# One more recurrent step of the last two batches with seven products instead of eight, and a new planned order

## The chip, the core and the metric

The kernel runs on one core of a Trainium2 chip. The metric is the device time of one execution in microseconds (us). The kernel before was timed three times: 1460.43, 1460.33 and 1458.93 us, median 1460.33. One further execution was recorded by the hardware profiler.

## The reference

Sixteen batches of 1024 nodes with 128 features pass two layers, each with a residual and a layer norm. Layer 0 is an attention layer over a fixed 0/1 adjacency matrix; layer 1 is a gated recurrent network of five steps on the same matrix. Cut to what matters here:

```python
# layer 0
h = x @ others_weight
att = softmax(where(adj > 0, leaky_relu(u1[pairs] + u2[pairs]), NEG), axis=1)
x = layernorm(x + att @ h + x @ self_weight)
# layer 1: five times, h starts as x
m  = adj @ h                               # per batch, 1024 x 1024 by 1024 x 128
u  = h @ u3.T
z  = sigmoid([m, m] @ w3.T + u);  r = sigmoid([m, m] @ w4.T + u)
hv = tanh([m, m] @ w5.T + (r * h) @ u5.T)
h  = (1 - z) * h + z * hv
# end
out = layernorm(x + h)
```

## The kernel before

Everything lies in halves of 128 x 512 floats: `hT` is the state of a batch, features on the partitions and nodes along a row, in two halves. The batches go in pairs, q = 0 to 7. The work of pair q and step s is one *message* stage and then *gates*.

**Messages (from L1045).** They need the state with nodes on the partitions, split in two parts that TensorE multiplies one after the other: a rounded part (`split`, the cast at L609 on ScalarE) and the rest (the subtraction at L613 on VectorE). One product is eight matmuls of 128 x 512 (L621). A *plain* stage makes eight products for a pair. A stage in *Strassen's form* makes seven, out of sums of the four halves of both batches (L1083) and of four sums of the adjacency's quarters, which were made once; both batches of the pair are then needed at once, and their results are put together by copies on ScalarE (L1141, L1143) and additions on VectorE (L1151). The set `PLAIN` at L28 lists the plain stages as (pair, step).

**Gates (from L1163).** For each half of each batch: a matmul of the state (L1189), a copy of it (L1192), two matmuls of the message (L1199) for r and z, their tanh (L1202), r times the state (L1209, VectorE), two matmuls for the candidate (L1215, L1216), its tanh (L1221), and three VectorE operations, less, times and sum (L1224, L1227, L1230), the last of which writes the state. All these matmuls are in float32.

**Leaving a step (from L1283).** The new state must be turned. Either TensorE does it, four transposes of 128 x 128 for a half (L571), and the split reads PSUM; the set `TURNED` at L32 lists the (pair, step) for which this is so. Or VectorE turns blocks of 32 x 32 (L579), four DMAs write the half to DRAM in the right places (`away`, L589), and one DMA brings it back (`back`, L597). After the last step the half gets the input added (L1332 or L1262) and is normalised.

**A norm (L522).** Statistics on VectorE (L527, L529), four or five small operations on GpSimd with the power -1/2 (L533 to L543), and four scalings on ScalarE (L548).

**The order.** No engine decides it while the program runs. The class `Plan` records every piece of work with its engine, a length in ns, a rank and the tiles that it reads and writes. `order` then plays the work through once: an engine that is free takes the ready piece of lowest rank. What follows from a piece is ready after its length and a *lag*, which stands for semaphores and, for a DMA, for the time to landing. The instructions are issued in the order that comes out; each engine, and the queue of DMAs on SyncE, works through its own list strictly in turn. Ranks are `10 * pair + 4.2 * step` plus an offset by kind of work, from the table `D` at L303; a batch before its first step has `rank0` at L317. `LATE` (L31) is the lag of the DMA that brings a half back. `LATER` (L29) sets the second batch of the last pair back by 1.5 in plain stages only. So a changed lag or offset moves instructions on every engine.

Of the kernel before, what the change touches and what calls it, by code (L numbers as in the profile page):

```python
# [24 lines left out]
SHIFT = 40.0  # L25
LOW, HIGH = -20.0, 100.0
TINY = 1e-30
PLAIN = {(0, 0), (0, 1), (0, 2), (7, 2), (7, 3), (7, 4)}  # L28
LATER = 1.5  # L29
AHEAD = range(4, 8)  # L30
LATE = 3001  # L31
TURNED = {(0, 0), (0, 1), (7, 2), (7, 3)}  # L32
IDLE = 60


# [102 lines left out]
def kernel(  # L138
# [79 lines left out]
    def exact(pools):  # L218
# [67 lines left out]
        plan = Plan({tag: k[0] for tag, k in kinds.items()})  # L286
# [13 lines left out]
            plan.add("SP", *a, **k)  # L300


        D = dict(m=-0.8, pu=1.4, u=0.8, pr=0.8, pz=1.2, r=1.7, pv=1.0, z=1.3, hv=-0.4, h=1.2, tr=1.6, o=6.6, ln=2.9)  # L303
        D.update(out=4.4, l1=-9, l2=-4, l3=-2, l4=-4, l5=-7, l6=-1.5, l7=-1, l8=-2)

        def on_pe(b, what):

# [7 lines left out]
            return 10 * (b // 2) + 4.2 * s + (LATER if b == B - 1 and plain(b // 2, s) else 0)  # L315

        def rank0(b):  # L317
            return 10 * (b // 2) - 1 * (1 - b % 2) + -1.0 - 6 * (b // 2 == 1)

        def sign(b):  # L320

            return 1 if b % 2 else -1
# [17 lines left out]
        def early_loads():  # L340
# [28 lines left out]
            writes=[(boot, "early"), (ws, "early"), (x0, "early"), (("xt", 1), "early"), *((t, "early") for k in staged for t in k)],  # L369
# [149 lines left out]
                dve(V, 1 + c / 4, sum_, reads=[*y, *more], writes=[(("tab",), c, n)])  # L519


        def layernorm(key, g, rank, after, src, dst, write, sg=1, short=False, later=()):  # L522
            stats, mv, rstd = ("stats", *key, g), ("mv", *key, g), ("rstd", *key, g)

            def look():
                for j in range(4):
                    nc.vector.bn_stats(T(stats)[:, j, :], src(j))  # L527
                for j in range(4):
                    nc.vector.bn_aggr(T(mv)[:, j, :], T(stats)[:, j, :])  # L529

            def power():
                mean, var, r = T(mv)[:, :, 0], T(mv)[:, :, 1], T(rstd)
                nc.gpsimd.tensor_scalar(r[:, 0, :], var, EPS, None, ALU.add)  # L533
                nc.gpsimd.tensor_tensor(r[:, 0, :], r[:, 0, :], mhalf[:, 0:4], ALU.pow)
                if short:
                    if sg < 0:
                        nc.gpsimd.tensor_scalar(r[:, 0, :], r[:, 0, :], -1.0, None, ALU.mult)
                elif sg > 0:
                    nc.gpsimd.tensor_scalar(r[:, 1, :], mean, -1.0, None, ALU.mult)
                    nc.gpsimd.tensor_tensor(r[:, 1, :], r[:, 1, :], r[:, 0, :], ALU.mult)  # L540
                else:
                    nc.gpsimd.tensor_tensor(r[:, 1, :], mean, r[:, 0, :], ALU.mult)
                    nc.gpsimd.tensor_scalar(r[:, 0, :], r[:, 0, :], -1.0, None, ALU.mult)  # L543

            def scale():
                r = T(rstd)
                for j in range(4):
                    nc.scalar.activation(  # L548
                        dst(j), src(j), AF.Identity, bias=r[:, 1, j : j + 1], scale=r[:, 0, j : j + 1]
                    )  # L550

            def scale_short():
                for j in range(4):
                    nc.vector.tensor_scalar(
                        dst(j), src(j), T(mv)[:, j, 0:1], T(rstd)[:, 0, j : j + 1], ALU.subtract, ALU.mult
                    )

            after = after if isinstance(after, list) else [after]
            dve(1100, rank, look, reads=after, writes=[(stats, 0), (mv, 0)])
            plan.add("POOL", 2301 if short else 3001, rank, power, reads=[(mv, 0)], writes=[(rstd, 0)])  # L560
            if short:
                dve(900, rank, scale_short, reads=[*after, (mv, 0), (rstd, 0)], writes=[write])
            else:
                act(1250, rank, scale, reads=[*after, *later, (mv, 0), (rstd, 0)], writes=[write])
# [66 lines left out]
        def layer0(b):  # L631

            first = rank0(b) - (60 if b == 0 else 0)
            rank = first + D["l1"]
            xt, hx, pb, u, us, uu, ud = (
                ("xt", b), ("hx", b), ("pb", b), ("u3", b), ("us", b), ("uu", b), ("ud", b)
            )
# [6 lines left out]
            yT, y0, yd = ([(k, b, g) for g in range(2)] for k in ("yT", "y0", "yd"))  # L644
# [46 lines left out]
            if b >= 2:  # L691
# [6 lines left out]
                    reads=[(u, 0), (u, 1), (("ident",), 0)],  # L698
                    writes=[(put, 0)],
# [8 lines left out]
                    reads=[(us, 0)],  # L708
                    writes=[(ud, 0)],
# [5 lines left out]
                    reads=[(ud, 0)],  # L715
                    writes=[(pb, 0), (pb, 1)],
                    lag=3000,
# [245 lines left out]
            for g in range(2):  # L963
                rank = rank0(b) + D["l5"]

                def y(g=g):
                    return T(yT[g])

                t = ("ps", "t", b, "y", g)
                if on_pe(b, "y"):  # L970
                    transposes(y, [(yT[g], 0)], t, rank)
                else:
                    k, d, t = (x + (b, "y", g) for x in (("T",), ("D",), ("F",)))
                    turn(k, y, [(yT[g], 0)], rank)
                    away(k, d, rank)
                    back(d, t, rank)

                def src(j, t=t, flat=on_pe(b, "y")):
                    return T(t)[:, j * P : (j + 1) * P] if flat else chunks(T(t))[:, j]

                def dst(j, g=g, flat=on_pe(b, "y")):
                    c = T(y0[g])[:, j, :]
                    return c if flat else c.rearrange("p (a j) -> p a j", a=4)

                layernorm(("y", b), g, rank0(b) + D["l6"], (t, 0), src, dst, (y0[g], 0), sign(b))

            if not plain(b // 2, 0):

# [293 lines left out]
        def leave(b, s):  # L1282

            rank = rank_of(b, s)
            hT = ("hT", b)
            for g in range(2):

                def h(g=g):
                    return T(hT)[:, g * HALF : (g + 1) * HALF]

                k, d = ("T", b, s, g), ("X", b, s + 1, g)
                if s < STEPS - 1 and on_pe(b, s):
                    t = ("ps", "t", b, s, g)
                    transposes(h, [(hT, g)], t, rank + D["tr"])
                    split(
                        ("blk", b, "h", s + 1, g),
                        lambda t=t: T(t).rearrange("p (c a j) -> p c a j", c=4, a=4),
                        [(t, 0)],
                        rank_of(b, s + 1),
                    )  # L1300
                    continue
                if s < STEPS - 1:
                    turn(k, h, [(hT, g)], rank + D["tr"])
                    away(k, d, rank + D["tr"])
                    continue

                if b >= B - 2:
                    end(b, s, g, h, rank)
                    continue

                t = ("ps", "t", b, s, g)
                if on_pe(b, s):
                    transposes(h, [(hT, g)], t, rank + D["tr"])
                else:
                    t = ("F", b, s, g)
                    turn(k, h, [(hT, g)], rank + D["tr"])
                    away(k, d, rank + D["tr"])
                    back(d, t, rank + D["o"])

                o, yd = ("o", b, g), ("yd", b, g)  # L1320
                sp(
                    450,
                    rank + D["o"],
                    lambda o=o, yd=yd: nc.sync.dma_start(T(o).rearrange("p c d -> p (c d)"), T(yd)),
                    reads=[(yd, 0), (hT, g)],
                    writes=[(o, "y")],
                )

                def last(t=t, o=o, flat=on_pe(b, s)):
                    x = T(o).rearrange("p c (a j) -> p c a j", a=4)  # L1330
                    n = T(t).rearrange("p (c a j) -> p c a j", c=4, a=4) if flat else chunks(T(t))
                    nc.vector.tensor_tensor(x, n, x, ALU.add)  # L1332

                dve(V, rank + D["o"], last, reads=[(t, 0), (o, "y")], writes=[(o, "raw")])

                def at(j, o=o):
                    return T(o)[:, j, :]

                layernorm(("o", b), g, rank + D["ln"], (o, "raw"), at, at, (o, 0), sign(b))
                plan.add(  # L1340
                    "POOL",
                    900,
                    rank + D["out"],
                    lambda o=o, g=g: nc.gpsimd.dma_start(
                        out[b].rearrange("(c p) d -> p c d", p=P)[:, 4 * g : 4 * g + 4, :], T(o)
                    ),
                    reads=[(o, 0)],
                    writes=[((o, "sent"), 0)],
                    lag=2600,
                )  # L1350
# [347 lines left out]
```

## Time and profile before

| | |
|---|---|
| median of three timed executions | 1460.33 us (1458.93 to 1460.43) |
| the profiled execution, whole time | 1468.01 us |
| its span, first to last instruction | 1466.2 us |
| TensorE idle in the span | 25.8 us |
| of it before 40 us | 3.1 us |
| of it after 1440 us | 13.4 us |
| TensorE clock granted, mean | 0.994 |
| norms: powers on GpSimd | 64, two for each batch and layer |

The profiled execution took 7.68 us longer than the median of the timed ones, and 1.8 us of it lie outside its span. A busy TensorE in this profile means a chain of matmuls without a gap between them: one product of eight matmuls advances it by 1.87 us, a float32 matmul of 128 x 512 by 0.86 us (two records), four transposes by 0.43 us. Where one instruction follows another in a view of the timeline, the difference of the starts is the time that counts, since the records of neighbours overlap.

### The profile page before, as it was taken

To read this page: it belongs to the slowest core of one execution; us is meant where nothing else is said; L and a number is where in the kernel's file an instruction comes from. 1 tells how busy PE (TensorE), PEld (TensorE's weight loads), DVE (VectorE), ACT (ScalarE), POOL (GpSimd) and SP (SyncE) were. 2 spreads that over 40 slices of the span, in tenths; PEclk is the share of its full clock that TensorE was granted. 3 is DMA by queue.
4 is the path that set the end of the run, shared out by engine and by line. 5 is a ranking of instruction groups with operands and counts; after the bars stand their busy time and mean duration, and the time that the engine had idled before them with its cause. 6 is when DMAs were issued, how large, how long until landed. Compare 5 with 4: busy or idle time off the path is not lost.

```text
span 1466.2 us, 17789 instructions
## 1 busy us (share of the span) xinstructions
PE 1440.4 (98%) x5020; PEld 902.3 (62%) x5020; DVE 1160.1 (79%) x2753; ACT 896.2 (61%) x1792; POOL 203.3 (14%) x323
## 2 busy tenths in 40 slices
PE   9999999998999999999999999999999999999996
PEld 7766656665566656666666656656566656556663
DVE  5997789868888789987888788896988877776535
ACT  5656465665657665666657576566655656664544
POOL 0311001012101150110201112011200123000201
PEclk9999999999999999999999999999999999999998
DMA  7426135554434643455434543445432554223201
GB/s 250 145 55 205 52 102 150 137 158 116 112 100 137 184 126 90 121 163 150 108 108 123 158 129 101 115 143 159 123 89 79 150 166 129 58 72 87 72 0 31
DMA packets 188032, 174.20 MB, mean 119 GB/s; under 512 B 34239, under 2 KB 137366, under 8 KB 187926
## 3 DMA queue, kind: packets, MB, share of 16 engines
q1 hardware_dynamic: 182562, 156.41, 37.8%
q0 software_dynamic: 4800, 15.73, 3.2%
q8 instruction: 41, 0.67, 0.2%
q10 hardware_dynamic: 564, 0.85, 0.2%
q14 instruction: 65, 0.53, 0.1%
HBM read 95.68 MB, written 77.24 MB: 118 GB/s over the span
## 4 chain that ended last, share of the span: by engine, by line
PE 88%; DVE 4%; DMA 2%; SPq 1%; ACT 1%; issue 1%; POOL 1%; DVEq 0%; POOLq 0%; ACTq 0%
PE ps_acc_a L621 16%; PE ps_g_r L1199 8%; PE ps_g_v L1215 8%; PE ps_g_v L1216 8%; PE gz L1199 8%; PE ps_g_r L1189 8%; PE ps_acc_c L621 8%; PE ps_acc_po L621 8%; PE ps_acc L621 5%; PE gz L621 4%; PE ps_g_ph L658 1%; PE ps_idle L419 1%; SPq L589 1%; PE ps_acc_px L925 1%; PE ps_acc_po L939 1%
## 5 line engine op out<-in xcount | busy, mean ns | idle before, releaser
L1215 PE MATMUL ps_g_v<-m,wm 128*128 128x512 f32 x320 | 163.5, 592 | 0.1
L1216 PE MATMUL ps_g_v<-r,u5h 128*128 128x512 f32 x320 | 163.4, 592 | 0.0
L1199 PE MATMUL ps_g_r<-m,wm 128*128 128x512 f32 x320 | 160.0, 593 | 2.6 <-ACT gz L1192 2.6
L1199 PE MATMUL gz<-m,wm 128*128 128x512 f32 x320 | 159.5, 592 | 0.0
L1189 PE MATMUL ps_g_r<-hT,u 128*128 128x512 f32 x320 | 153.3, 592 | 0.0
L1224 DVE TENSOR_TENSOR hv<-hv,hT 128x512 f32<-128x512 f32 x160 | 109.8, 686 | 51.5 <-ACT hv L1221 51.0
L621 PE MATMUL ps_acc_a<-tab,blk_s 128*128 128x512 f32 x544 | 148.6, 415 | 1.6 <-ACT m L1141 1.6
L1209 DVE SCALAR_TENSOR_TENSOR r<-r,hT 128x512 f32<-128x512 f32 x160 | 109.2, 685 | 51.3 <-ACT r L1202 51.0
L1202 ACT ACTIVATE r<-ps_g_r,bh 128x512 f32<-128x512 f32 x160 | 109.1, 687 | 66.4 <-PE ps_g_r L1199 66.1
L621 PE MATMUL ps_acc_po<-adj,blk 128*128 128x512 f32 x512 | 141.5, 423 | 0.0
L1202 ACT ACTIVATE z<-gz,bh 128x512 f32<-128x512 f32 x160 | 109.6, 687 | 24.5 <-PE gz L1199 24.0
L621 PEld LDWEIGHTS ps_acc_a<-tab,blk_s 128*128 128x128 f32 x544 | 101.1, 188 | 37.5 <-issue 11.1
L621 PEld LDWEIGHTS ps_acc_po<-adj,blk 128*128 128x128 f32 x512 | 95.9, 188 | 36.6 <-issue 12.5
L1230 DVE SCALAR_TENSOR_TENSOR hT<-hv,hT 128x512 f32<-128x512 f32 x160 | 108.7, 681 | 2.2
L1227 DVE SCALAR_TENSOR_TENSOR hv<-z,hv 128x512 f32<-128x512 f32 x160 | 108.4, 678 | 2.1 <-ACT z L1202 1.1
L1192 ACT COPY gz<-ps_g_r 128x512 f32<-128x512 f32 x160 | 91.0, 572 | 29.7 <-PE ps_g_r L1189 28.2
L533 POOL TENSOR_SCALAR rstd_y<-mv_y 128x4 f32<-128x4 f32 x32 | 13.5, 422 | 682.1 <-DVE mv_y L529 657.6
L1216 PEld LDWEIGHTS ps_g_v<-r,u5h 128*128 128x128 f32 x320 | 60.6, 189 | 76.8 <-issue 61.1
L1199 PEld LDWEIGHTS gz<-m,wm 128*128 128x128 f32 x320 | 60.5, 190 | 76.4 <-issue 76.4
L621 PE MATMUL ps_acc<-adj,blk_h 128*128 128x512 f32 x384 | 101.3, 414 | 0.0
L609 ACT CAST blk_s<-G 128x512 fp32r<-128x512 f32 x136 | 82.3, 617 | 30.8 <-DVE G L1083 29.2
L613 DVE TENSOR_TENSOR blk_s<-G,blk_s 128x512 fp32r<-128x512 f32 x136 | 92.0, 681 | 8.7 <-ACT blk_s L609 8.2
(191 smaller groups left out, 2595.4 us busy)
## 6 DMA issues: line engine op xcount, KB each, us to landing
G<-X SPq DMA_DIRECT2D x140, 256.0 KB, 2.9
X<-T SPq DMA_DIRECT2D x552, 64.0 KB, 1.8
yd<-y POOLq DMA_DIRECT2D x32, 256.0 KB, 3.3
D_y<-T_y SPq DMA_DIRECT2D x112, 64.0 KB, 1.8
F_y<-D_y SPq DMA_DIRECT2D x28, 256.0 KB, 2.7
X<-y SPq DMA_DIRECT2D x28, 256.0 KB, 2.0
D_b<-T_b SPq DMA_DIRECT2D x112, 64.0 KB, 2.2
F_b<-D_b SPq DMA_DIRECT2D x28, 256.0 KB, 3.0
```

Source lines behind the costliest of these rows:

```text
L613: lambda: nc.vector.tensor_tensor(half(1), src(), half(0), ALU.subtract),
L621: nc.tensor.matmul(T(bank), T(blk)[:, k, c, :], right(c), start=(first and i == 0), stop=(last and i == len(terms) - 1), skip_group_check= ...
L1189: nc.tensor.matmul(T(pr), u3, h(), start=True, stop=True)
L1192: nc.scalar.copy(T(pz), T(pr))
L1199: nc.tensor.matmul(T(p_), wm[:, j, :], T(m), start=False, stop=True, skip_group_check=True)
L1202: nc.scalar.activation(T(t), T(p_), AF.Tanh, bias=bh[:, j : j + 1], scale=0.5 * sg)
L1209: lambda r=r, h=h: nc.vector.scalar_tensor_tensor(T(r), T(r), 1.0, h(), ALU.add, ALU.mult),
L1215: nc.tensor.matmul(T(pv), wm[:, 2, :], T(m), start=True, stop=False)
L1216: nc.tensor.matmul(T(pv), u5h, T(r), start=False, stop=True)
L1224: nc.vector.tensor_tensor(T(hv), T(hv), h(), ALU.subtract)
L1227: nc.vector.scalar_tensor_tensor(T(hv), T(z), 1.0, T(hv), ALU.add, ALU.mult)
L1230: nc.vector.scalar_tensor_tensor(h(), T(hv), 0.5, h(), ALU.mult, ALU.add)
```

## The change

The third step of the last pair, (7, 2), leaves `PLAIN`, so that it is in Strassen's form. (0, 1) and (7, 2) leave `TURNED`, so that after these two stages the state is turned by VectorE and two trips through DRAM. `LATE` falls from 3001 to 2601 ns. The norms get a parameter `calm`, the plan's lag after the power on GpSimd in place of 200 ns: 1201 ns for the first norm of batches 4 and up, 4001 ns for the second norm of all batches but the last two. Seven offsets of rank and the early rank of the second pair change. `calm`, `LATE` and the ranks are numbers of the plan alone: they add no instruction and no wait, they change the order.

```diff
-PLAIN = {(0, 0), (0, 1), (0, 2), (7, 2), (7, 3), (7, 4)}
+PLAIN = {(0, 0), (0, 1), (0, 2), (7, 3), (7, 4)}
 LATER = 1.5
 AHEAD = range(4, 8)
-LATE = 3001
-TURNED = {(0, 0), (0, 1), (7, 2), (7, 3)}
+LATE = 2601
+TURNED = {(0, 0), (7, 3)}
...
-        D = dict(m=-0.8, pu=1.4, u=0.8, pr=0.8, pz=1.2, r=1.7, pv=1.0, z=1.3, hv=-0.4, h=1.2, tr=1.6, o=6.6, ln=2.9)
-        D.update(out=4.4, l1=-9, l2=-4, l3=-2, l4=-4, l5=-7, l6=-1.5, l7=-1, l8=-2)
+        D = dict(m=-0.6, pu=1.4, u=0.8, pr=0.4, pz=1.2, r=1.7, pv=1.0, z=0.9, hv=-0.4, h=1.2, tr=1.6, o=6.6, ln=3.3)
+        D.update(out=4.4, l1=-9, l2=-4, l3=-2, l4=-4, l5=-5, l6=-1.5, l7=-1, l8=-2)
...
-            return 10 * (b // 2) - 1 * (1 - b % 2) + -1.0 - 6 * (b // 2 == 1)
+            return 10 * (b // 2) - 1 * (1 - b % 2) + -1.0 - 2 * (b // 2 == 1)
...
-        def layernorm(key, g, rank, after, src, dst, write, sg=1, short=False, later=()):
+        def layernorm(key, g, rank, after, src, dst, write, sg=1, short=False, later=(), calm=None):
...
-            plan.add("POOL", 2301 if short else 3001, rank, power, reads=[(mv, 0)], writes=[(rstd, 0)])
+            plan.add(
+                "POOL", 2301 if short else 3001, rank, power, reads=[(mv, 0)], writes=[(rstd, 0)], lag=calm
+            )
...
-                layernorm(("y", b), g, rank0(b) + D["l6"], (t, 0), src, dst, (y0[g], 0), sign(b))
+                layernorm(("y", b), g, rank0(b) + D["l6"], (t, 0), src, dst, (y0[g], 0), sign(b), calm=1201 if b >= 4 else None)
...
-                layernorm(("o", b), g, rank + D["ln"], (o, "raw"), at, at, (o, 0), sign(b))
+                layernorm(("o", b), g, rank + D["ln"], (o, "raw"), at, at, (o, 0), sign(b), calm=4001)
```

## The prediction

> **What bounds the kernel now.** I read the page first, then TensorE's waits, then the timeline at each of these waits and at the end of the program.
>
> ```profile
> PE 1440.4 (98%) x5020; PEld 902.3 (62%) x5020; DVE 1160.1 (79%) x2753; ACT 896.2 (61%) x1792; POOL 203.3 (14%) x323
> ...
> PE 88%; DVE 4%; DMA 2%; SPq 1%; ACT 1%; issue 1%; POOL 1%; DVEq 0%; POOLq 0%; ACTq 0%
> ```
>
> TensorE is busy for 98% of the span and carries 88% of the chain that ended last. Time can come only from fewer matmuls or from its few gaps.
>
> ```profile
> PE ps_acc_a L621 <- ACT m L1143: 4.4, 1, 4.4
> PE ps_t L571 <- DVE hT L1230: 3.0, 3, 1.5
> PE ps_g_r L1199 <- ACT gz L1192: 2.6, 2, 1.7
> ...
> PE ps_acc_a L621 <- ACT m L1141: 1.6, 2, 1.1
> ```
>
> In the middle of the program there are four gaps: 4.37 us at 341.6, 1.72 at 531.1, 0.52 at 547.2 and 1.10 at 1205.9, 7.7 us in all. The timeline shows what lies behind the first:
>
> ```profile
> 332.30 4.78 POOL L533 TENSOR_SCALAR rstd_o<-mv_o 128x4 f32<-128x4 f32 x1 [29.03 <-DVE mv_o L529]
> ...
> 336.91 0.71 DVE L579 STREAM_TRANSPOSE T<-hT 128x512 f32<-128x512 f32 x1
> ...
> 338.85 1.65 ACT L548 ACTIVATE o<-o,rstd_o 128x128 f32<-128x128 f32 x4 [5.46 <-POOL rstd_o L543]
> ...
> 341.60 3.59 PE L621 MATMUL ps_acc_a<-tab,blk_x 128*128 128x512 f32 x8 [4.37 <-ACT m L1143]
> ```
>
> A GpSimd operation that mostly takes 0.2 to 0.6 us took 4.78, so ScalarE stood 5.46 us before a norm's scaling, with the copy that TensorE needed behind it. The gaps at 531 and 547 have the same origin (L533 of 4.18 and 2.99 us). The one at 1205.9 is a DMA that landed late. After the first gap eight matmuls took 3.59 us, not 1.87:
>
> ```profile
> 341.60:345.20 3.60, 3.60 (x9) 2.82 (x10) 3.53 (x10) 1.18 (x3) 0.04 (x1) 0.53 0.28 84
> ```
>
> The granted clock (third value from the end) was 0.53, so that gap cost 1.7 us more. With it the middle loses 9.4 us.
>
> The stage that the change rebuilds has no gap before. Its states are turned on TensorE between products:
>
> ```profile
> 1354.47 0.60 PE L571 MATMUL ps_t<-ident,hT 128*128 128x128 f32 x4
> 1354.83 2.09 PE L621 MATMUL ps_acc<-adj,blk_h 128*128 128x512 f32 x8
> 1356.76 0.60 PE L571 MATMUL ps_t<-ident,hT 128*128 128x128 f32 x4
> ```
>
> The way through DRAM, as the previous step of this pair takes it:
>
> ```profile
> 1312.59 0.70 DVE L579 STREAM_TRANSPOSE T<-hT 128x512 f32<-128x512 f32 x1
> ...
> 1313.32 1.78 SPq L589 DMA_DIRECT2D X<-T  x4
> ...
> 1316.60 0.34 SPq L597 DMA_DIRECT2D G<-X  x1
> ...
> 1319.73 0.61 ACT L609 CAST blk_h<-G 128x512 fp32r<-128x512 f32 x1
> ```
>
> From the end of the turn to the second DMA's issue: 3.3 us; the page gives 2.9 us from there to landing; cast, subtraction and semaphores are 1.5. Before it come the tanh (0.9 with its semaphore), three VectorE operations that wait for each other (0.72 each in the last gates, from 1450.06) and the turn, 3.8 us. So from the end of L1216 to the first product that uses the half, 12.0 us at best.
>
> [...] GpSimd went on as the turn at 336.91, with one input, began. [...]
>
> **The change, part by part.**
>
> *Fewer matmuls.* (7, 2) has seven products, not eight: 1.87 us less. Leaving (0, 1) and (7, 2) without TensorE takes off 8 groups of four transposes at 0.43 us: 3.4. Together -5.3 us of TensorE work, in stages where it is the bound. The added sums, turns and combinations on VectorE and 20 DMA issues for each of the two stages lie beside TensorE in the middle; what they cost where cover is thin comes next.
>
> *The tail, (7, 2) to (7, 3).* Before, pair 6 fills this place; after its last step nothing else is left. In the changed program's instruction order, count from T, the end of L1216 for batch 14, half 0. TensorE then has three L1189 (to 2.6), four L1199 (6.0), the candidate of 14 half 1 (7.7), one L1199 (8.6), the candidate of 15 half 0 (10.3), one L1199, L1215 of 15 half 1 (12.0), its L1216 (12.9), and then the products of batch 14: two with half 0 and two with half 1.
> Half 0: tanh and three operations 3.05, an addition of the output norm in between 0.6, turn 0.7: T+4.35. First DMAs 7.65, landed 10.55, cast 11.15. This cast stands on ScalarE ahead of the tanh of 15 half 0, which ends at 11.85 for that reason. VectorE then has, in this order, less (15), sum (14), times (15), turn (14), sum (15), and L1209 of 15 half 1: six at 0.6 us, end near 15.6. L1216 waits for that: 3.7 us of gap against 12.0. The subtraction for half 0 follows one turn later: 0.45 more. For half 1 the turn ends at 14.4, but on SyncE's queue the four DMAs of batch 15 stand ahead of the one that brings it back, so that is issued at 18.0, landed at 20.9, split at 22.4; TensorE is there at 20.7: 1.7. Sum 5.9 us. The lower bound is 3.1 (12.0 needed against 8.9 of TensorE work between for half 1), the upper 7.5 if a load of the output norm holds SyncE. A gap of 3.7 us may or may not halve the clock (0 or 1.7); I take 0.5. Tail: +6.4.
>
> *The start.* The second pair's layer 0 is ranked four later, so fewer of its matmuls lie between the first norms and the transposes that need them: 6.5 to 7.2 us of TensorE work where the trace of before had 8.4 to 9.3, and a norm takes 6.2 to 6.5 with free engines. I take 0.6. For (0, 1) to (0, 2) the four halves have 12.7 to 14.7 us against 12.0, while on SyncE loads for batches 4 and 6 that wait for TensorE to free their tiles stand between: 0.7. Start: +1.3, bounds 0 and 4.
>
> *The later powers.* With `calm` the scalings stand about 4 us later on ScalarE, so a power of up to 7 us blocks nothing; what is late next is the scaled output, which only leaves for DRAM. In the profile this is worth the three gaps and the clock, 8.3 us. But the sum must be set against the timed runs. The profile is 7.68 us above their median, and float32 matmuls in it advance by 0.43 us a record without a gap, so TensorE's work can hardly be what is shorter without the profiler; the start's 3.1 us of gaps cannot make up all of it. I conclude that most of the middle's 9.4 us are not in the timed runs, and take 9.4 - 7.7 = 1.7 us as what can be cured there. Bounds 0 and 9.4.
>
> *`LATE` and the new order.* The plan now counts 450 + 2601 ns for a return that takes 2.9 us and a semaphore, so ScalarE's casts stand with no margin, where it had 0.4 us. All 1,240 rows of TensorE's order are planned again. The TensorE work between a producer and its user hardly differs: at least 16.6 us from a candidate to the next stage's first products, before 17.8; at least 0.96 us around a copy of an accumulator, before 0.86. I take 2.5 us for gaps like those at 547 and 1206, bounds 0 and 6.
>
> *Sum*: -5.3 - 1.7 + 6.4 + 1.3 + 2.5 = +3.2 us on the timed median: 1463.5. Against the profile, where the cure counts 8.3, it is -3.4: its 1468.0 would become 1464.6.
>
> **Rivals.**
>
> *The gaps behind GpSimd are in the timed runs too* (faster). For it: VectorE's order is fixed[...]. Against: the 7.68 us. It decides from a cure of 4.9 us on, since that is what the rest of the sum adds. In full, 9.4 in place of 1.7: 1455.8.
>
> *The new order costs nothing* (no change). The plan's order left 7.7 us of gaps in 1,400 us before, so it is good at this; then start and middle give back 3.8 us: 1459.7. Against: less work lies between in the start, and no margin for returns.
>
> *A shorter tail* (a part of the forecast's range). If ScalarE could take the tanh of batch 15 ahead of the cast, only the bound of 3.1 us would be left there, and the time would be near 1460.5.
>
> **How the numbers follow.** About 0.2% (2.9 us) can be told from no change. Forecast 0.52 (own range 1460 to 1469), first rival 0.28, second 0.20. Faster: 0.22 from the first rival, 0.04 from the second, 0.01 from the forecast. Same: 0.11, 0.06 and 0.10. Slower: 0.40 from the forecast, 0.06 from the second rival should `LATE` cost its upper bound. The range 1453 to 1470 takes in the first rival and the upper bounds.
>
> **What will show it.** The tail: in the profile after, L1216 waits for L1209 by 3 to 4.5 us between 1350 and 1390, and a product for L613 by 1 to 3 us. GpSimd: no gap over 1 us on TensorE behind L548. TensorE's busy time falls by 5 to 7 us. I am wrong if the tail has no gap over 2 us, or if the timed median falls by the size of the cured gaps.

## The result, and the profile after

The changed kernel is slower: 1466.74 us (median of 8; 1462.45 to 1472.24) against 1460.38 (1457.91 to 1461.82), ratio 1.0044, 95% interval 1.0030 to 1.0058. In us that is +6.4 (4.4 to 8.5); the forecast was +3.2. Its profiled execution took 1467.15 us, 0.4 above its median, where that of before lay 7.6 above.

The page after, engines and chain of work:

```profile
PE 1436.7 (98%) x4980; PEld 898.5 (61%) x4980; DVE 1172.5 (80%) x2770; ACT 903.6 (62%) x1796; POOL 194.3 (13%) x323
...
PE 90%; DMA 4%; DVE 2%; SPq 1%; issue 1%; ACT 1%; POOL 0%; DVEq 0%; POOLq 0%
```

TensorE has forty instructions fewer and is busy for 3.7 us less. TensorE's waits after (total, times, longest):

```profile
PE ps_g_v L1218 <- DVE r L1211: 7.2, 3, 4.1
```

From L560 on the line numbers of before are two higher here: L1218 is L1216 there, L1211 is L1209. The waits behind the norms' scalings are gone from the middle: between 175 and 1340 us one gap of 0.34 us is left of 7.7. Instead there are two gaps in the tail, the only ones between 1340 and 1400. The timeline there:

```profile
1366.84 0.69 DVE L1334 TENSOR_TENSOR o<-ps_t,o 128x512 f32<-128x512 f32 x1 [2.17 <-DMA o<-yd]
...
1367.45 0.70 DVE L581 STREAM_TRANSPOSE T<-hT 128x512 f32<-128x512 f32 x1
...
1369.81 1.12 PE L1218 MATMUL ps_g_v<-r,u5h 128*128 128x512 f32 x2 [1.17 <-DVE r L1211]
...
1370.06 0.38 SPq L1326 DMA_DIRECT2D o<-yd  x1
...
1372.78 0.69 DVE L1334 TENSOR_TENSOR o<-ps_t,o 128x512 f32<-128x512 f32 x1 [2.42 <-DMA o<-yd]
...
1374.22 0.62 ACT L611 CAST blk_h<-G 128x512 fp32r<-128x512 f32 x1 [1.71 <-DMA G<-X]
...
1374.75 0.68 ACT L1223 ACTIVATE hv<-ps_g_v,b 128x512 f32<-128x512 f32 x1
...
1375.62 0.68 DVE L1226 TENSOR_TENSOR hv<-hv,hT 128x512 f32<-128x512 f32 x1
...
1378.62 0.68 DVE L1211 SCALAR_TENSOR_TENSOR r<-r,hT 128x512 f32<-128x512 f32 x1
...
1379.36 2.08 PE L1218 MATMUL ps_g_v<-r,u5h 128*128 128x512 f32 x2 [4.13 <-DVE r L1211]
```

Read it from the top: VectorE stands 2.17 us before an addition of the output norm whose load has not landed, and the turn of batch 14 half 0 is next in its queue. So the half goes out late and its cast comes late (1374.22); the tanh of batch 15 half 0 is queued behind the cast and ends at 1375.43. At the same time a second load of the output norm stands in SyncE's queue behind the half's four DMAs (it is issued at 1370.06), and VectorE stands another 2.42 us before the addition that needs it. From that addition on VectorE has no pause, and it comes to the first operation that needs the tanh at 1375.62, 0.2 us after the tanh has ended. So two delays meet there, and the trace doesn't tell what each alone would have cost. L1211 is the sixth operation from there, and TensorE's L1218 waits 4.13 us. What the gap does to the clock is seen in the stretch behind it (stretch, length, busy and number of matmuls, granted clock, DMA share, GB/s):

```profile
1379.36:1383.40 4.04, 4.04 (x8) 0.50 0.90 239
1383.40:1390.63 7.23, 7.23 (x28) 0.85 0.42 112
```

The float32 matmul (two records) and the 32 of the four products take 11.27 us from 1379.36 to 1390.63; at full clock they take 8.33, worked out from the advances in the profile of before. So the tail costs 5.30 us of gaps and 2.9 of slow clock, 8.2 in all. The third gap that was forecast, for half 1, is not there: that half landed while the slow products ran.

The start after:

```profile
145.12 0.43 DVE L1375 TENSOR_SCALAR junk_look<-look 128x512 f32<-128x512 f32 x1 [2.59 <-DMA look<-in_adj_dram]
...
146.06 0.69 DVE L1211 SCALAR_TENSOR_TENSOR r<-r,hT 128x512 f32<-128x512 f32 x1
...
146.80 1.13 PE L1218 MATMUL ps_g_v<-r,u5h 128*128 128x512 f32 x2 [1.89 <-DVE r L1211]
...
155.72 0.49 PE L623 MATMUL ps_acc<-adj,blk_h 128*128 128x512 f32 x1 [0.68 <-ACT blk_h L611]
...
161.71 0.50 PE L623 MATMUL ps_acc<-adj,blk_h 128*128 128x512 f32 x1 [1.16 <-ACT blk_h L611]
```

From 140 to 175 us TensorE has gaps of 4.75 us, where before had one wait of 0.86 us, which ends at 140.2: 1.89 behind a load of the looks at the adjacency (the 0/1 check that is spread over the first layers), and 2.86 at 155 to 163, where products of (0, 2) wait for halves that came through DRAM.

By place, in the two profiles: TensorE work -5.3; start (to 175 us) +5.2; middle -7.4, and -1.7 of slow clock behind its first gap; tail +5.1 and +2.9 of clock. In the start each of the two has one stretch of slow clock that costs 1.7 us (3.41 us at 0.50, from 27.8 us before, from 163.6 after, behind the waits for the halves), which cancels. The sum is -1.2 us, and the profiled executions differ by -0.9. The timed runs differ by +6.4. So the two profiles don't carry the answer by themselves: some 7 us that the profile of before shows, most likely of the middle, are missing in its timed runs. That, and the size of each part, is what the experiments are for.

### The profile page after: what moved, and what is told of

Same layout as the page of the kernel before. It is cut to its first block, busy times and chain, and to the rows that moved or that the text cites. A ratio compares the mean times of both kernels' runs of the same rounds, so it can differ in the third digit from the quotient of the medians.

```text
span 1465.3 us, 17785 instructions
## 1 busy us (share of the span) xinstructions
PE 1436.7 (98%) x4980; PEld 898.5 (61%) x4980; DVE 1172.5 (80%) x2770; ACT 903.6 (62%) x1796; POOL 194.3 (13%) x323
## 4 chain that ended last, share of the span: by engine, by line
PE 90%; DMA 4%; DVE 2%; SPq 1%; issue 1%; ACT 1%; POOL 0%; DVEq 0%; POOLq 0%
PE ps_acc_a L623 17%; PE ps_g_r L1201 9%; PE ps_g_v L1218 9%; PE gz L1201 9%; PE ps_g_r L1191 9%; PE ps_g_v L1217 9%; PE ps_acc_c L623 9%; PE ps_acc_po L623 8%; PE gz L623 4%; PE ps_acc L623 4%; PE ps_g_ph L660 1%; DMA look<-in_adj_dram 1%; SPq L591 1%; PE ps_acc_px L927 1%; PE ps_acc_po L941 1%
## 5 line engine op out<-in xcount | busy, mean ns | idle before, releaser
L1218 PE MATMUL ps_g_v<-r,u5h 128*128 128x512 f32 x320 | 164.6, 596 | 7.2 <-DVE r L1211 7.2
L1211 DVE SCALAR_TENSOR_TENSOR r<-r,hT 128x512 f32<-128x512 f32 x160 | 109.1, 686 | 42.1 <-ACT r L1204 41.6
L623 PEld LDWEIGHTS ps_acc_a<-tab,blk_s 128*128 128x128 f32 x560 | 104.2, 188 | 31.7 <-issue 6.9
L1218 PEld LDWEIGHTS ps_g_v<-r,u5h 128*128 128x128 f32 x320 | 60.6, 190 | 84.9 <-issue 64.0
L581 DVE STREAM_TRANSPOSE T<-hT 128x512 f32<-128x512 f32 x146 | 102.6, 704 | 4.7 <-DMA X<-T 3.8
L611 ACT CAST blk_s<-G 128x512 fp32r<-128x512 f32 x140 | 85.3, 618 | 29.1 <-DVE G L1085 27.7
L533 POOL TENSOR_SCALAR rstd_y<-mv_y 128x4 f32<-128x4 f32 x32 | 14.2, 444 | 636.7 <-DVE mv_y L529 635.8
```

The source lines that it names most:

```text
L581: nc.vector.transpose(T(t).rearrange("p (b c i) -> p b c i", b=4, c=4), turned(src()))
L623: nc.tensor.matmul(T(bank), T(blk)[:, k, c, :], right(c), start=(first and i == 0), stop=(last and i == len(terms) - 1), skip_group_check= ...
L1211: lambda r=r, h=h: nc.vector.scalar_tensor_tensor(T(r), T(r), 1.0, h(), ALU.add, ALU.mult),
L1218: nc.tensor.matmul(T(pv), u5h, T(r), start=False, stop=True)
```

## The experiments

Ratios are to the kernel before, run on the same chip. The gaps are TensorE's idle times of the profiled execution that its timeline marks, summed from 5 to 175 us, from 175 to 1340, and from 1340 to 1400.

| kernel | ratio (95%) | median us | gaps: start, middle, tail |
|---|---|---|---|
| before | 1 | 1460.4 | 2.94, 7.71, 0.16 |
| after | 1.0044 (1.0030 to 1.0058) | 1466.7 | 8.10, 0.34, 5.30 |
| b_again: before | one execution, profiled | 1466.9 | 3.11, 8.41, 0.31 |
| b_calm: before, later powers | 0.9973 (0.9961 to 0.9984) | 1456.7 | 1.78, 0, 0 |
| a_no_calm: after without them | 1.0047 (1.0030 to 1.0063) | 1467.9 | 7.22, 3.04, 4.03 |
| a_tail_plain: after, (7, 2) plain | 1.0008 (0.9997 to 1.0018) | 1462.6 | 7.24, 0.63, 0 |
| a_start: that, (0, 1) turned on TensorE | 1.0045 (1.0030 to 1.0059) | 1466.3 | 6.05, 4.24, 0 |
| a_start_ranks: that, second pair's rank of before | 1.0001 (0.9991 to 1.0011) | 1460.8 | 4.84, 3.56, 0 |
| a_order: that, `LATE` of before | 1.0016 (1.0008 to 1.0025) | 1462.4 | 5.35, 2.27, 0 |
| a_pe_turn: after, (7, 2) turned on TensorE | 1.0008 (0.9998 to 1.0018) | 1461.7 | 6.83, 0.70, 0.73 |
| a_tail_load: after, loads of pair 6 reckoned later | 1.0041 (1.0026 to 1.0055) | 1466.3 | 7.59, 0.70, 5.35 |
| a_look_lag: after, looks reckoned later | 1.0061 (1.0048 to 1.0073) | 1469.8 | 7.74, 3.43, 5.44 |
| c_72: b_calm, (7, 2) Strassen | 0.9999 (0.9990 to 1.0007) | 1461.0 | 3.18, 0, 4.04 |
| c_01: b_calm, (0, 1) through DRAM | 1.0033 (1.0022 to 1.0045) | 1466.4 | 4.05, 3.32, 0 |

### Are the gaps behind GpSimd real? (b_again, b_calm, a_no_calm)

b_again is the kernel before with no edit.

> The kernel before, unchanged, profiled once more. Question: are its three gaps behind slow GpSimd powers (4.37 us at 341.6, 1.72 at 531.1, 0.52 at 547.2) a property of its fixed instruction order, or a chance of one execution? If they belong to the order, the second profile shows the same slow powers (L533 of 4.8, 4.2 and 3.0 us) and the same gaps within 0.5 us, and again a profiled execution near 1468. If they are a chance, some are missing or others stand in their place, and the profiled execution is shorter by what is missing (up to 9.4 us with the slow clock behind the first).

Measured: the same powers are slow by the same amounts, and the gap stands behind the first again.

```profile
330.83 4.78 POOL L533 TENSOR_SCALAR rstd_o<-mv_o 128x4 f32<-128x4 f32 x1 [29.57 <-DVE mv_o L529]
...
340.12 3.53 PE L621 MATMUL ps_acc_a<-tab,blk_x 128*128 128x512 f32 x8 [4.01 <-ACT m L1143]
```

The three slow powers took 4.78, 4.18 and 2.98 us, in the first profile 4.78, 4.18 and 2.99. They belong to the fixed order, and both executions with the profiler have them. It took 1466.89 us, again 5.2 above the median of the timed runs beside it.

b_calm puts the new lags into the kernel before:

```diff
...
-            plan.add("POOL", 2301 if short else 3001, rank, power, reads=[(mv, 0)], writes=[(rstd, 0)])
+            plan.add("POOL", 2301 if short else 3001, rank, power, reads=[(mv, 0)], writes=[(rstd, 0)], lag=calm)
...
-                layernorm(("y", b), g, rank0(b) + D["l6"], (t, 0), src, dst, (y0[g], 0), sign(b))
+                layernorm(("y", b), g, rank0(b) + D["l6"], (t, 0), src, dst, (y0[g], 0), sign(b), calm=1201 if b >= 4 else None)
...
-                layernorm(("o", b), g, rank + D["ln"], (o, "raw"), at, at, (o, 0), sign(b))
+                layernorm(("o", b), g, rank + D["ln"], (o, "raw"), at, at, (o, 0), sign(b), calm=4001)
```

> The kernel before with the later reckoning of the norms' powers alone (both lags), all else as before, so TensorE has the same 1440 us of work. Theory 1 (the prediction's): the profile loses the gaps behind L548, about 8 us, but the timed median falls by only 2 to 3 us, to about 1458, since most of those gaps are not in the timed runs. Rival (the prediction's first): the gaps are in the timed runs too, and the median falls by 8 to 9 us, to about 1452. Second rival: the new order that the lags bring costs as much as they cure, 1460.

Measured: 0.9973, or 3.9 us faster (2.3 to 5.7), and the fastest kernel of the study. Its profile has no gap between 140 and 1400 us; one view of it (stretch, length, TensorE busy and number of matmuls, granted clock, DMA share, GB/s):

```profile
400.00:800.00 400.00, 400.00 (x1354) 1.00 0.47 129
```

The profiled execution fell by 11.9 us against b_again, the timed runs by 3.9. The 8 to 9 us of the first rival are excluded, and 3.9 lies above the 2 to 3 of theory 1, of which the interval still allows the larger part. So a cure of these gaps is worth less than half of what the profile shows, even at the upper end of the interval (5.7 of 11.9). Why an execution without the profiler has less of them isn't shown.

a_no_calm takes the lag out of the changed kernel (`lag=None` in place of `lag=calm`).

> The changed kernel without the later reckoning of the norms' powers, the rest of the change kept. Theory 1: 2 to 3 us slower than the changed kernel in the timed runs, about 1469, and gaps behind L548 come back in the profile. Rival: the reckoning is worth 8 us, about 1475. Second rival: it is worth nothing without the gaps of before's own order, 1466.7, and the profile shows no GpSimd power over 2 us with a gap behind it.

Measured: 1.0047 beside 1.0044 for the changed kernel, a difference of 0.4 us with some 3 us of uncertainty either way. In that order the slowest GpSimd operation of a norm after 100 us takes 3.33 us, and the gaps of the middle sum up to 3.04 us. The time is the second rival's, but not its sign, that no power over 2 us would be seen. So what the lags are worth depends on the order that they meet: 3.9 us in the kernel before, nothing that can be told in the changed one.

### The tail (a_tail_plain, a_pe_turn, a_tail_load, c_72)

a_tail_plain:

```diff
-PLAIN = {(0, 0), (0, 1), (0, 2), (7, 3), (7, 4)}
+PLAIN = {(0, 0), (0, 1), (0, 2), (7, 2), (7, 3), (7, 4)}
...
-TURNED = {(0, 0), (7, 3)}
+TURNED = {(0, 0), (7, 2), (7, 3)}
```

> The changed kernel with the third step of the last pair back in the plain form and turned on TensorE (the tail undone), the rest of the change kept; the order before that step stays the same. Theory 1: the tail's two gaps (1.17 and 4.13 us) and the slow clock behind them (2.9 us) go, eight matmuls (1.87 us) and four groups of transposes (1.7 us) come back: 4.6 us faster than the changed kernel, about 1462. Rival: the tail costs nothing net and the loss lies in the start and the new order, so the time stays within 1 us of 1466.7 or rises by up to 3.6 us.

Measured: 1.0008, 5.3 us faster than the changed kernel (2.6 to 7.9, from the two intervals), and no gap between 1340 and 1400. The 8.2 us that were read from the profile less the 3.6 of added work make 4.6: the tail's cost is in the timed runs at about its full size, and it is 5.3 of the loss of 6.4. The two kernels issue the same instructions in the same order on every engine up to 1314 us.

a_pe_turn keeps Strassen's form and leaves out only the way through DRAM:

```diff
-TURNED = {(0, 0), (7, 3)}
+TURNED = {(0, 0), (7, 2), (7, 3)}
```

> The changed kernel, Strassen's form kept at the third step of the last pair, but its states turned by TensorE and not through DRAM. Theory 1: the tail's loss is the way through DRAM: the gaps of 1.17 and 4.13 us and the slow clock (2.9 us) go, but for up to 1 us; four groups of transposes (1.7 us) come back: 5.5 to 6.5 us faster than the changed kernel, about 1460.5, and 1.9 faster than the plain form with turns on TensorE. Rival: Strassen's form itself delays the gates (L1218 waits for L1211 with the turns on TensorE too): faster by no more than 3 us, 1464 or above.

Measured: 1.0008. The two waits for halves in the tail are now of 0.38 and 0.35 us:

```profile
1378.38 0.50 PE L623 MATMUL ps_acc<-adj,blk_h 128*128 128x512 f32 x1 [0.38 <-ACT blk_h L611]
...
1379.23 1.90 PE L623 MATMUL ps_acc<-adj,blk_h 128*128 128x512 f32 x7 [0.35 <-DVE blk_h L615]
```

With the turns on TensorE no L1218 waits in the tail, so it was the trip and what queues up behind it, not Strassen's sums, that delayed the gates. The order is that of the changed kernel up to the first of these turns, at 1365 us. No turn of these states stands in VectorE's list here, so none can be held up there behind a load, and TensorE has products with half 0 to go on with. 5.3 us of the expected 5.5 to 6.5 came. The 1.9 us by which it should beat the plain form are not seen, as the ratio is the same; the trace leaves 1.1 us (1.87 less 0.73 of gaps), which the runs, with some 2 us of uncertainty, can't tell from nothing.

a_tail_load asks how much of it is VectorE's queue:

```diff
-                    writes=[(o, "y")],
+                    writes=[(o, "y")], lag=5001 if b in (12, 13) else None,
```

> The changed kernel, with one thing altered in the plan: the loads of pair 6's unnormalized output are reckoned to land 2.5 us later, so that VectorE's queue has the turn of batch 14 half 0 ahead of the addition that waits for such a load (it stood 2.17 us before it), and L1211 of batch 15 half 1 five places earlier. The way through DRAM stays. Theory 1: both waits of L1218 go (5.3 us); half 0 is there in time; the products with half 1 then wait 3 to 4.5 us for its landing, so the tail still costs 4 to 6 us of the 8.2: 2 to 4 us faster than the changed kernel, about 1464. Rival: the queue's order was all of it, no wait over 1 us is left between 1350 and 1390 and it is 7 to 8 us faster, about 1459.

Measured: 1.0041, no change that can be told. Both waits of L1218 are gone, and the same length is lost in one piece:

```profile
1364.28 0.71 DVE L581 STREAM_TRANSPOSE T<-hT 128x512 f32<-128x512 f32 x1
...
1371.16 0.68 DVE L1211 SCALAR_TENSOR_TENSOR r<-r,hT 128x512 f32<-128x512 f32 x1
...
1374.23 0.70 DVE L581 STREAM_TRANSPOSE T<-hT 128x512 f32<-128x512 f32 x1
...
1374.96 4.77 SPq L591 DMA_DIRECT2D X<-T  x8
...
1379.89 0.34 SPq L599 DMA_DIRECT2D G<-X  x1
...
1382.63 0.62 ACT L611 CAST blk_h<-G 128x512 fp32r<-128x512 f32 x1 [6.15 <-DMA G<-X]
...
1383.30 8.27 PE L623 MATMUL ps_acc<-adj,blk_h 128*128 128x512 f32 x24 [5.35 <-ACT blk_h L611]
```

Counted from the same matmul, the turn of half 0 is 2.7 us earlier and L1211 7.0. The products with half 0 run without a wait. But half 1 is turned at 1374.23, and on SyncE's queue four DMAs of batch 15, which had to wait for their own turn, stand ahead of the one that brings it back: from the end of the turn to the cast are 7.7 us. TensorE waits 5.35 us, and its 24 matmuls then take 8.27 us where 5.6 are full clock (0.70 was granted), so the slow clock is paid as well. This is the third gap of the forecast, in the place where it was put, once the first no longer hides it. The expectation of 2 to 4 us was wrong: the wait for half 1 was put at 3 to 4.5 and its clock left out.

c_72 sets the form of a_pe_turn into b_calm:

```diff
-PLAIN = {(0, 0), (0, 1), (0, 2), (7, 2), (7, 3), (7, 4)}
+PLAIN = {(0, 0), (0, 1), (0, 2), (7, 3), (7, 4)}
```

> The kernel before with the later powers (0.9973) and the third step of the last pair in Strassen's form, its states turned on TensorE as before. Theory 1: one product less (1.87 us) against gaps of about 0.7 us in the tail: 1 us faster than with the later powers alone, 0.9965, about 1455.5. Rival: as in the changed kernel, where both forms with turns on TensorE gave 1.0008, the sums and combinations take back what the product gives: 0.9973 or above, about 1457.

Measured: 0.9999, 3.8 us slower than b_calm (1.7 to 5.9).

```profile
1370.92 0.69 DVE L1332 TENSOR_TENSOR o<-ps_t,o 128x512 f32<-128x512 f32 x1 [1.52 <-DMA o<-yd]
1371.52 0.68 DVE L1230 SCALAR_TENSOR_TENSOR hT<-hv,hT 128x512 f32<-128x512 f32 x1
...
1372.35 0.63 PE L571 MATMUL ps_t<-ident,hT 128*128 128x128 f32 x4 [2.16 <-DVE hT L1230]
...
1375.10 3.20 PE L621 MATMUL ps_acc<-adj,blk_h 128*128 128x512 f32 x7 [1.88 <-DVE blk_h L613]
```

Here too a load of the output norm holds VectorE, this time with the last sum of a state behind it. The two gaps are 4.04 us, and the seven matmuls behind them take 3.20 us, not 1.64: 5.6 us lost. Less the 1.87 of the product that makes 3.7, where 3.8 was measured. Up to 1306 us the order is that of b_calm. In a_pe_turn, with the new ranks, the same form has only 0.73 us of gaps here, so this price lies in the order, not in the form.

### The start and the ranks (a_start, a_start_ranks, a_order, a_look_lag, c_01)

a_start, from a_tail_plain:

```diff
-TURNED = {(0, 0), (7, 2), (7, 3)}
+TURNED = {(0, 0), (0, 1), (7, 2), (7, 3)}
```

> The changed kernel with the tail undone as in the run before and, on top, the turn of (0, 1) back on TensorE. Against that run (1.0008 of the kernel before). Theory 1: the four waits for a half that comes through DRAM at 155 to 163 us (0.68, 0.46, 1.16, 0.56 in the profile of the changed kernel, 2.9 us in all) and part of the wait of L1218 for L1211 at 147 (1.9) go, four groups of transposes (1.7 us) come back: 1 to 3 us faster, about 1460. Rival: the start's waits come from the second pair's new rank, not from the way through DRAM; then only the 1.7 us of transposes are added, and the waits at 140 to 175 stay: about 1464.

Measured: 1.0045, 5.4 us slower than a_tail_plain (2.6 to 7.9). Even the rival allowed for only 1.7. The waits for halves at 155 to 163 are gone, a wait of 1.72 us for a copy of ScalarE stands at 153, and the middle of the new order has gaps of 4.24 us where a_tail_plain has 0.63. So the rest of the program, planned anew, cost more than the place that was edited gave. The gaps and the transposes make 4.1 us of it. The two profiled executions don't show the loss (1465.72 here, 1466.05 for a_tail_plain): that of a_tail_plain loses 6.8 us to slow clock before 175 us (0.94 was granted from 20 to 80 us, 0.90 from 140 to 175), the other none (1.00 in both), and its execution lies 3.5 us above its own median.

a_start_ranks, from a_start:

```diff
-            return 10 * (b // 2) - 1 * (1 - b % 2) + -1.0 - 2 * (b // 2 == 1)
+            return 10 * (b // 2) - 1 * (1 - b % 2) + -1.0 - 6 * (b // 2 == 1)
```

> As the run above, and the second pair's layer 0 ranked as before, so that of the change only the later powers, the shorter counted return and the new ranks in D are left. Theory 1: 1 to 2 us faster than the run above (no wait over 1 us between 20 and 175), near the kernel before with the later powers alone (0.9973 of before), about 1458. Rival: the shorter return and the ranks in D cost the 2.5 us that were forecast for them, so it stays at 1460 or above, with waits of products for blk_h in the middle.

Measured: 1.0001, 6.4 us faster than a_start (3.8 to 9.0), and 140 to 175 us has no gap. The profiled executions differ by 4.8 us, of which 1.9 are gaps and 1.8 TensorE's busy time; the rest isn't resolved there. It still lies 4.1 us behind b_calm.

a_order, from a_start_ranks: `LATE = 3001` in place of 2601.

> As the run with the ranks of before (1.0001 of before), and the counted return back at 3001 ns: of the change only the later powers and the new ranks in D are left. Theory 1 (the margin for returns costs): a third or more of the 4 us by which that run is behind the later powers alone (0.9973) comes back, about 1458, and the wait of a product for blk_h at 130.8 (1.27 us) goes. Rival: the ranks in D cost them; no change within 1 us, gaps of 1 to 1.5 us of L1217 and L1201 behind ScalarE's copies stay.

Measured: 1.0016, 2.2 us slower than with the shorter return, at the edge of what can be told. The wait for blk_h is still there, 1.00 us at 132.9. The rival is right as to the cause: the ranks in `D` cost 6.3 us here against b_calm, and no cost of the lost margin for returns is seen.

a_look_lag, from the changed kernel:

```diff
-                writes=[(a, 0)],
+                writes=[(a, 0)], lag=5001,
```

> The changed kernel, the loads of the looks at the adjacency reckoned to land 2.5 us later in the plan, nothing else altered (the tail and the later return of the change stay). Question: is the loss at 140 to 175 that the second pair's rank brought VectorE's standing before such loads (2.18 and 2.59 us in the profile of the changed kernel, L1211 behind the second)? Theory 1: then the wait of L1218 for L1211 at 147 (1.89 us) goes and with it 2 to 3 us of the time, about 1464; the waits for halves through DRAM at 155 to 163 (2.9 us) stay. Rival: the start's loss is the crowded queue of DMAs, and VectorE's order only shows it: another wait of 1 to 2 us takes its place, and the time stays within 1 us of 1466.7.

Measured: 1.0061, 2.5 us slower than the changed kernel, with 2.7 us of uncertainty, so no change that can be told. L1218 no longer waits at 147, and the time is lost some 11 us later:

```profile
158.07 0.62 ACT L611 CAST blk_h<-G 128x512 fp32r<-128x512 f32 x1 [2.24 <-DMA G<-X]
...
158.75 1.52 PE L623 MATMUL ps_acc<-adj,blk_h 128*128 128x512 f32 x2 [2.58 <-ACT blk_h L611]
```

Two waits for ScalarE of 0.89 and 0.88 us stand just ahead of it. Together 140 to 175 us has gaps of 4.35 us, where the changed kernel has 4.75, and the slow clock behind them is longer: 64 matmuls from 158.75 take 18.15 us, not the 14.9 that the 1.87 of a product give (0.90 was granted from 140 to 175 us). So the rival holds in that other waits took the place of the one that went, and curing the look gave nothing. That the crowded queue of DMAs is what bounds this stage is argued, not shown; the halves' wait was to stay by theory 1 too. The middle of its order has 3.1 us more of gaps, one of them of 2.52.

c_01, from b_calm:

```diff
-TURNED = {(0, 0), (0, 1), (7, 2), (7, 3)}
+TURNED = {(0, 0), (7, 2), (7, 3)}
```

> The kernel before with the later powers (0.9973) and the step (0, 1) turned through DRAM, the second pair ranked as before. Theory 1: where the second pair keeps its rank its work covers the trip, so the waits for blk_h stay under 1 us and the four groups of transposes (1.7 us) are saved: 0.9962 to 0.9973, about 1455.5. Rival: the trip costs what it costs in the changed kernel, where the products of (0, 2) wait 2.9 us: 0.998 or above, about 1458.

Measured: 1.0033, 8.8 us slower than b_calm (6.4 to 11.2). The halves make TensorE wait at 153 to 168 (2.44 us in four gaps, and L1216 0.51 us just ahead of them), although the second pair has its old rank; the slow clock behind the first two costs 1.7 us more (0.95 was granted from 140 to 175 us). In the middle one wait costs twice:

```profile
372.22 3.26 PE L621 MATMUL ps_acc_a<-adj,blk_x 128*128 128x512 f32 x7 [2.40 <-DVE blk_x L613]
```

Seven such matmuls take 1.64 us at full clock, seven eighths of a product: this gap of 2.40 us cost another 1.6. All gaps up to 1400 us are 5.6 us more than in b_calm and the slow clock 3.3; less the 1.7 of transposes that makes 7.2 of the 8.8.

## Why the prediction was right, and where it was off

**Put together.** From before to after in five steps, each one pair of neighbouring runs, in us of 1461:

| step | runs | us |
|---|---|---|
| later powers | before, b_calm | -3.9 ± 1.7 |
| ranks in `D`, `LATE` | b_calm, a_start_ranks | +4.1 ± 2.2 |
| rank of the second pair | a_start_ranks, a_start | +6.4 ± 2.6 |
| (0, 1) through DRAM | a_start, a_tail_plain | -5.4 ± 2.6 |
| tail: (7, 2) Strassen through DRAM | a_tail_plain, after | +5.3 ± 2.6 |

The sum is +6.4 by construction. Only the tail's number stands for its edit alone, since the order is the same on every engine up to 1314 us. Each of the others plans most of TensorE's order again, and the sign is not fixed: (0, 1) through DRAM gave 5.4 us in one order and cost 8.8 in another.

**Direction.** Slower, as forecast: 4.4 to 8.5 us, inside the range. That the tail loses by the way through DRAM is shown by a_pe_turn, whose order differs only from that point on. That the sum came so near is partly luck. By the profiles the tail was 1.8 us and the start 3.9 us too small, 5.7 together, while only 3.2 are missing; so by this reckoning the later powers and the new order, +0.8 in the forecast, make about -1.7.

**Fewer matmuls, -5.3.** The count is right (5020 to 4980 records: eight matmuls of a product and 32 transposes). Busy time fell by 3.7, not by 5 to 7, because the slow clock behind the tail's gap counts as busy: -5.3 of work, -1.7 of before's slow stretch gone, +2.9 of a new one, -4.1 in all.

**Tail, +6.4.** This is the term that was mis-sized most clearly: 8.2 by the profile of the changed kernel. L1218 waited for L1211 by 4.13 us (forecast 3.7), and the cast ahead of the tanh and the six operations up to L1211 came in the order that was described. But that chain alone didn't set the time: VectorE's second stand before a load, 2.42 us, brought it to the first of the six 0.2 us after the tanh. The wait of 1.17 us was not foreseen. The step that failed is the same for both: the addition of the output norm was priced at its length of 0.6 us, while the first waits 2.17 us for its load and the second 2.42. The 2.15 us for the two halves' products did not appear, since the slow clock covered them; a_tail_load shows the one for half 1. And the clock, taken at 0.5, cost 2.9. The bounds of 0 and 1.7 for it were too narrow: 1.7 was read from a slow stretch of 3.4 us, and here it lasts 6.8, from 1378.70 to 1385.53. The terms for the way from L1216 to the next product add up to 11.5 us (3.8, 3.3, 2.9 and 1.5), not to the 12.0 that was written; that makes the tail's lower bound 2.6 and changes nothing else that matters. The shorter tail of the third rival didn't come. No run takes the tanh ahead of the cast, its remedy; in this order VectorE was not free before the tanh anyway, and VectorE's better order in a_tail_load only moved the wait.

**Start, +1.3.** Too small: gaps of 8.10 us where before has 2.94, and with the waits of L455 at 27 to 28 us left out, which vary from kernel to kernel (2.26 after, 1.73 before), it is still 4.6 more, above the upper bound of 4. The wait at 63.4 was 0.90, forecast 0.6. The trip from (0, 1) to (0, 2) cost 2.9 of waits, forecast 0.7, and 1.7 of slow clock behind them, forecast nothing; c_01 has 2.4 and 1.7 with the old rank. The estimate had counted loads on SyncE alone; that the second pair's casts and looks in the queues of ScalarE and VectorE make up the rest is argued, as no run takes them out alone. The wait of L1218 at 147 was not foreseen at all.

**Later powers, -1.7.** The lags alone gave 3.9 us, and in the changed order nothing that can be told. The reading that the profile overstates the gaps is shown, by b_again and b_calm together. As to which part of 9.4 us can be cured, 1.7 was too little for the kernel before. The place named in advance holds: no gap behind L548 over 1 us in the middle.

**`LATE` and the new order, +2.5.** `LATE` is not a cost: putting it back made the kernel slower (a_order). The ranks cost 4.1 us together with it. In a_start_ranks the middle has gaps of 3.56 us, 1.71 of them before products that wait for copies of messages, as at 547 and 1206, and the start has 3.1 us more than in b_calm, which was not named. But in the changed kernel's own middle there is a gap of 0.34 us only. So the term has about the size of what the ranks cost without the rest of the change, is wrong as to `LATE`, and isn't found in the changed kernel.

**The rivals.** The first needed a cure of 4.9 us; alone it is 3.9, inside the change less. The second, an order that costs nothing, is refuted: b_calm and a_start_ranks have the same work and differ by 4.1 us. The sum came out on the right side with two terms too small and one, the cost of the new order, that is not found in the changed kernel's middle.

## What to carry to other kernels

When a plan is made anew with each edit, an edit costs what the whole new order costs: measure it alone and in combination, and sum up gaps by stage before you believe either. Before a trip through memory is put into a stage, count the work that covers the latest half, its wait in the queue of DMAs behind other transfers included (7.7 us from the turn to the cast in a_tail_load); price an operation that waits for a load by its wait, not by its length (2.17 and 2.42 us here, against 0.6); and mending the order at the first visible wait can move the loss to the next one, as it did here (gaps of 5.30 us in the tail became 5.35 in a_tail_load). Of this change the later powers alone are worth keeping: 1456.7 us, faster than both kernels.

## What the runs showed of the hardware

Three GpSimd operations (L533) of the kernel before took the same time in two profiled executions, to 0.01 us: 4.78 and 4.78, 4.18 and 4.18, 2.99 and 2.98, where the median of the 32 in the second norms is 0.52. In the first of the two profiles VectorE began nothing but operations with two inputs beside each of them, until a turn, with one input, began at 336.91, 525.65 and 541.57; each of the three ended 0.2 us after that. The times thus belong to the order, and still the timed executions had less than half of their effect (3.9 us against 11.9). No run takes VectorE's operations away from beside them, so that these are the cause is not shown.

In the profile of before ScalarE kept to its list in turn: the copy for which TensorE waits ran at 340.97, after the scaling that had stood for 5.46 us, though by the profile the product that it copies had ended at 335.07.

The forecast's 0 or 1.7 us for the slow clock for a gap of 3.7 was the author's estimate; the profile of before has gaps on either side of it, one of 4.37 us, after which the next 3.60 ran at 0.53, and one of 1.72 us at 531.1, after which the next 3.87 ran at 1.00. More are measured now. The clock fell after 2.40 us in c_01, where 372 to 378 us ran at 0.72, and after 2.70 in a_tail_plain, where the next 4.8 us ran at 0.64. It fell after 1.73 us in the kernel before, too (0.50 from 27.82 us), and after 1.16 and 0.56 us with one matmul between in the changed one (0.50 from 163.55). After 2.52 us in a_look_lag eight matmuls took 1.97 us, near the 1.87 of a product at full clock. The stretches behind the gaps in c_01 and a_tail_plain, and the gap in a_look_lag:

```profile
372.00:378.00 6.00, 5.78 (x17) 0.72 0.64 141
...
150.20:155.00 4.80, 4.77 (x10) 0.64 0.40 117
...
718.95 2.12 PE L623 MATMUL ps_acc_a<-tab,blk_s 128*128 128x512 f32 x8 [2.52 <-ACT m L1143]
```

So no single length of a gap separates the gaps with a slow stretch behind them from those without, and what does isn't shown. Between 20 and 1440 us the profiles of before and after have two stretches at 0.50 each: 3.41 us from 27.82 and 3.41 from 341.85 before, 3.41 from 163.55 and 6.83 from 1378.70 after. An estimate follows from these lengths, for a TensorE that is busy all through: a stretch of 3.41 us costs 1.7 us, one of 6.83 us up to 3.4 (2.9 in the tail of the changed kernel). What makes one last twice as long isn't shown.
